# The last row's last local feed-forward and the return of the local stream, as pieces of the last layer's attention part

## The chip, the cores and the metric

The kernel runs on one core of a Trainium2 chip. The metric is the device time of one execution in microseconds (us), of which the median of several runs is taken; lower is better. A traced execution gives the span of the core's instructions and the rows that are quoted here. Engines: PE is TensorE (PEld its weight loads), DVE is VectorE, ACT is ScalarE, POOL is GpSimd, SP is SyncE, which here only issues DMAs.

## The reference

The program is four layers on a residual `x` of shape (4, 512, 128): each adds a cross attention to a context of 77 tokens and then a feed-forward of its own kind. The change touches the feed-forward of layer 2, which is a local transformer of six layers (`DEPTH`), and the cross attention of layer 3 behind it. Cut to what matters:

```python
def attn_layer(x, Wqkv, qs, ksc, Wo): ...      # 16 heads of 64, windows of 32 tokens

def ffn_layer(x, g, bln, W1, b1, W2, b2):
    mu = x.mean(-1, keepdims=True)
    var = ((x - mu) ** 2).mean(-1, keepdims=True)
    xn = (x - mu) / jnp.sqrt(var + 1e-05) * g + bln
    hg = xn @ W1 + b1                           # 128 -> 2 * 341
    a, gate = jnp.split(hg, 2, -1)
    return a * jax.nn.gelu(gate, approximate=False) @ W2 + b2

# _L2_ffn_ref, y = layernorm(x)
for i in range(6):
    y = attn_layer(shift_tokens(y), ...) + y
    y = ffn_layer(shift_tokens(y), ...) + y
x = x + y

# layer 3
x = x + cross_attention(layernorm(x), ctx)      # 16 heads of 8, 77 keys
x = x + routed_experts(layernorm(x))            # 8 experts, the best 2 for each token
```

`shift_tokens` moves the upper 64 features of every token by one token.

## The kernel before, in words

**Data.** A *row* is one of the 4 batch entries `b`. `x[b]` holds a row token-major: 128 partitions of tokens, `NT` = 4 tiles, 128 features. The local transformer keeps its own stream `Y[b]` feature-major, 128 features by 513 columns; its upper 64 features stand one column to the right, so that a slice from column 0 is the shifted stream and a slice from column 1 the unshifted upper half. `middle_part` fills `Y` from the normalised `x`. After the local transformer, `x` receives `Y` back, turned.

**Local transformer** (`local_transformer`). Its order is written out by hand, under `manual_schedule`: a pipeline over 96 tiles (layer, row, tile of 128 tokens), in which pass `n` does the projections of tile `n`, the scores of tile `n-1` and the averages of tile `n-2`. The feed-forward of a row (`ff_stage`) is spread over four passes: moments and normalisation (`ff_moments`, `ff_norm`), turning and gates (`ff_turn`, `ff_gate`), the other half (`ff_up`), and the down product with its add into `Y` (`ff_down`, `add_y` L1717). The row of number `m` has passes `n = 4m + 6` to `4m + 9`. The loop runs 10 passes beyond the 96 tiles. The last two tiles are finished in passes 96 and 97; row 3 of layer 5 (the last) has its feed-forward in passes 98 to 101, when no tile is left. Then a loop over the four rows turns `Y[b]` back with PE in two halves (L2108, 64 features each, since they differ by a column) and DVE adds each half to `x[b]` (L2111).

**Last part** (`last_part`). It is planned: `plan.add` records pieces with what they depend on, the buffers and PSUM banks that they take and use, and a cost for each engine that may do them. `Plan.run` then lists them, always the piece that can start first, the longest path first among equals, and picks the engine where there is a choice. The result is one fixed order per engine; an engine runs its instructions in this order and waits where one isn't ready. `context` forms the keys and values of layer 3 (L636, L649, L640, L657), `cross_attention` goes over the four rows: normalisation (`norm` L535 to L551, transposes L569), queries L684, scores L699 and L704 and their maxima L712, transposes of the maxima L729 and `shift` L738, logits L756 and L758, exponentials L764, the sums `total` L774, the weighted values L783, the projection and the residual L838. `Routing.row` places the tokens with the experts and sends them by indirect DMAs that POOL issues (L1018). In the same plan SP loads the expert weights (L1646 to L1648), and DVE splits `b2` into three bf16 terms (L322 to L329).

Each phase opens its own PSUM pool (`banks`), whose eight banks come free when the phase before has done with them. SBUF pools close with their phase: a later tile may lie where an earlier one was, and then waits for its last user. Before, `Y`'s pool closes with the local transformer, and the tiles of `open_cross` lie over it.

Of the kernel before, what the change touches and what calls it, by code (L numbers as in the profile page):

```python
# [29 lines left out]
NT = S // 128  # L30
# [209 lines left out]
def tile_kernel(ctx: ExitStack, tc: tile.TileContext, A: dict, out: bass.AP):  # L240
# [45 lines left out]
    def p_tr(*shape):  # L286
        return psum(shape, "tr", 2)
# [14 lines left out]
    def copy(e, dst, src):  # L302
        (e.copy if e is SC else e.tensor_copy)(dst, src)
# [223 lines left out]
    def norm(plan, b, after, dst, name, twice=False):  # L527
# [5 lines left out]
        def find(e):  # L533
            for t in range(NT):
                e.bn_stats(st.t[:, t], x[b][:, t])  # L535
            for t in range(NT):
                e.bn_aggr(mv.t[:, t], st.t[:, t])
# [10 lines left out]
        def apply(e):  # L548
            d = dst.t if isinstance(dst, Slot) else dst
            for t in range(NT):  # L550
                e.tensor_scalar(  # L551
                    d[:, t], x[b][:, t], mv.t[:, t, 0:1], rs.t[:, t : t + 1],
                    ALU.subtract, ALU.mult,
                )

        p = plan.add(find, after, takes=[st, mv], V=124)
        p = plan.add(inverse, [p], takes=[rs], uses=[mv], G=135)
        takes = [dst] if isinstance(dst, Slot) else []
        return plan.add(apply, [p], takes=takes, uses=[mv, rs], V=112, G=175)
# [1068 lines left out]
    def last_part():  # L1628

        with ExitStack() as es:  # L1630
# [6 lines left out]
            with tc.tile_pool(name="xw3", bufs=2) as wp, planned() as plan:  # L1637
                keys = context(plan, wp, 2)
                done = cross_attention(plan, wp, 2, keys, [[]] * B)
# [56 lines left out]
    def local_transformer(Y):  # L1696
        with ExitStack() as es:
# [28 lines left out]
            def load(i):  # L1726
# [16 lines left out]
                w1 = wp.tile([128, 2 * DI], F32, name="lw1")  # L1743
                DMA.dma_start(w1, A["L2_ffn_W1"][i])
                w2 = wp.tile([128, 3, D], F32, name="lw2")
# [217 lines left out]
            def ff_turn(F):  # L1963
# [7 lines left out]
                F.h = tp.tile([128, 3, S], F32, name="fh", bufs=1)  # L1971
# [62 lines left out]
            for n in range(len(tiles) + 10):  # L2034
# [66 lines left out]
                if F:  # L2101
                    ff_stage(F, phase, True)

            for b in range(B):
                for r, o in ((slice(0, 64), 0), (slice(64, 128), 1)):
                    t = p_tr(128, NT, 64)
                    for tt in range(NT):
                        PE.transpose(  # L2108
                            t[:, tt], Y[b][r, 128 * tt + o : 128 * tt + o + 128], ident[r, r]
                        )  # L2110
                    V.tensor_tensor(x[b][:, :, r], x[b][:, :, r], t, ALU.add)  # L2111

    with tc.tile_pool(name="y", bufs=1) as yp:
# [9 lines left out]
        local_transformer(Y)  # L2123
    with ExitStack() as es:
        open_cross(es)
        last_part()
# [19 lines left out]
```

## Time and profile before

| | us |
|---|---|
| median of 3 runs | 2501.84 |
| lowest and highest | 2493.18, 2504.8 |
| profiled execution, whole | 2497.58 |
| its span | 2495.8 |
| local transformer, first to last projection (L1780) | 533.7 to 2150.7 |
| row 3's feed-forward of layer 5, from its first transposes | 2188.47 to 2211.86 |
| `Y` turned back, up to the first product of `context` | 2211.87 to 2216.27 |
| attention part of layer 3, to the last row's residual | 2216.27 to 2352.95 |
| mean granted clock of PE over the span | 0.951 |

Times of rows are microseconds from the start of the span. A row of a stage has the stretch, its length, the busy time of PE, PEld, DVE, ACT and POOL with instruction counts, the granted PE clock as a share of full speed, the busy share of the DMA engines, and GB/s. A row of the chain of waits has start, length and what the chain went through. One of the timeline has start, length, engine, line, operation, output and inputs, and in brackets the idle time before it with what ended it. An fp32 matmul counts as two instructions on PE.

### The profile page before, as it was taken

The numbers are of one execution on the slowest core, as the hardware profiler recorded it, in microseconds if no ns is written. First come the engines' busy times: TensorE is split into PE (matmuls) and PEld (weight loads), VectorE is DVE, ScalarE is ACT, GpSimd is POOL, SyncE is SP. The second block draws the span as 40 slices with busy tenths as digits, with TensorE's granted clock in tenths as the row PEclk, the third lists the DMA queues.
The fourth block names the chain that finished last, engine by engine and source line by source line (L and its number), as shares of the span: only waits on it lengthen the run. The fifth ranks groups of instructions, "written<-read, shape, count | busy, mean of one in ns | idle before, by whom it ended". The sixth has DMA issues, their size and how long they took to land.

```text
span 2495.8 us, 86737 instructions
## 1 busy us (share of the span) xinstructions
PE 2257.5 (90%) x37341; PEld 1487.1 (60%) x37341; DVE 1746.9 (70%) x3818; ACT 1292.4 (52%) x2379; POOL 1383.5 (55%) x1948
## 2 busy tenths in 40 slices
PE   7959879968999999999999999999999999978676
PEld 3537644536666666666666666666666666634365
DVE  5526355757788787778888888788788888655522
ACT  3513225545666556666666666556556666524232
POOL 2241232347667666676667766766667666432433
PEclk9959889989999999999999999999999999979788
DMA  6210110014411121111211121111211111111022
GB/s 162 84 39 23 37 42 2 1 49 95 120 34 35 30 57 50 27 35 35 69 35 35 30 76 35 30 31 39 65 35 35 33 29 35 29 39 47 21 74 83
DMA packets 134297, 116.14 MB, mean 47 GB/s; under 512 B 29505, under 2 KB 102700, under 8 KB 133916
## 3 DMA queue, kind: packets, MB, share of 16 engines
q1 hardware_dynamic: 128373, 102.81, 15.8%
q0 software_dynamic: 4608, 7.35, 0.9%
q8 instruction: 296, 4.85, 0.8%
q14 instruction: 85, 0.70, 0.1%
q10 hardware_dynamic: 935, 0.43, 0.1%
HBM read 42.84 MB, written 21.52 MB: 26 GB/s over the span
## 4 chain that ended last, share of the span: by engine, by line
PE 72%; DVE 15%; issue 4%; ACT 3%; DMA 2%; POOL 2%; another core or an unknown queue 2%; SPq 1%; POOLq 0%; ACTq 0%; DVEq 0%
PE ps_tr L583 12%; PE ps_mm L1780 10%; PE ps_av L1942 6%; PE ps_av L1918 5%; PE ps_tr L1857 5%; PE ps_sc L1887 4%; DVE xn L523 3%; PE ps_sc L1977 3%; PE ps_sc L1988 3%; PE ps_sc L2000 2%; PE ps L774 2%; PE ps L1313 2%; PE ps L783 2%; PE ps L1682 2%
## 5 line engine op out<-in xcount | busy, mean ns | idle before, releaser
L1803 POOL TENSOR_TENSOR rc<-rc,rs 128x512 f32<-128x512 f32 x384 | 489.5, 1276 | 385.4 <-DVE rs L1793 329.5
L1780 PE MATMUL ps_mm<-wqk,y 128*128 128x512 f32 x768 | 396.9, 599 | 10.5 <-DVE rs L1793 7.3
L1822 POOL TENSOR_TENSOR rc<-rc,rn_y 128x512 f32<-128x512 f32 x384 | 388.7, 1044 | 7.5
L1790 DVE TENSOR_TENSOR rc<-ps_mm,tabs 128x512 f32<-128x512 f32 x384 | 262.5, 684 | 137.8 <-ACT sq L1782 123.4
L1782 ACT ACTIVATE sq<-ps_mm 128x512 f32<-128x512 f32 x384 | 231.4, 603 | 166.9 <-PE ps_mm L1780 119.3
L1793 DVE TENSOR_TENSOR rs<-ps_mm,tabs 128x512 f32<-128x512 f32 x384 | 261.5, 681 | 1.6 <-POOL rc L1803 1.4
L1802 DVE TENSOR_REDUCE ss<-sq 128x8 f32<-128x512 f32 x384 | 259.5, 676 | 0.0
L583 PE MATMUL ps_tr<-cst,rc 128*128 128x128 f32 x1536 | 210.7, 280 | 6.8 <-issue 4.1
L1918 PEld LDWEIGHTS ps_av<-v,PT 64*32 64x32 f32 x12288 | 138.1, 105 | 124.5 <-PE ps_tr L583 55.8
L1942 PE MATMUL ps_av<-aT,wo 128*128 128x128 f32 x1536 | 199.6, 283 | 3.4 <-issue 3.2
L1942 PEld LDWEIGHTS ps_av<-aT,wo 128*128 128x128 f32 x1536 | 181.0, 193 | 12.7 <-issue 4.0
L583 PEld LDWEIGHTS ps_tr<-cst,rc 128*128 128x128 f32 x1536 | 164.6, 141 | 26.7 <-issue 4.7
L1918 PE MATMUL ps_av<-v,PT 64*32 64x65 f32 x12288 | 169.9, 225 | 4.6 <-DVE attn L1928 2.1
L1887 PE MATMUL ps_sc<-kT,qT 64*32 64x64 f32 x12288 | 146.8, 224 | 28.9 <-issue 26.8
L1018 POOL DMA_INDIRECT back<-ye,to x80 | 78.0, 975 | 162.0 <-DVE ye L1132 120.4
L1887 PEld LDWEIGHTS ps_sc<-kT,qT 64*32 64x32 f32 x12288 | 140.1, 105 | 39.1 <-issue 31.4
L1780 PEld LDWEIGHTS ps_mm<-wqk,y 128*128 128x128 f32 x768 | 124.6, 192 | 60.7 <-issue 48.8
L764 ACT ACTIVATE P<-ps,deltaT 77x512 f32<-77x512 f32 x192 | 115.4, 682 | 77.5 <-PE ps L758 69.9
L1903 ACT ACTIVATE P<-P 128x1024 f32<-128x1024 f32 x96 | 101.5, 1057 | 92.1 <-DVE P L1898 92.1
L1814 ACT ACTIVATE rn_y<-ss 128x32 f32<-128x32 f32 x96 | 22.0, 229 | 238.4 <-POOL ss L1813 238.4
L1834 ACT COPY qT<-ps_tr 128x512 f32<-128x512 f32 x192 | 103.3, 589 | 74.6 <-PE ps_tr L583 74.3
L1834 ACT COPY kT<-ps_tr 128x512 f32<-128x512 f32 x192 | 103.3, 589 | 66.2 <-PE ps_tr L583 65.9
(394 smaller groups left out, 4439.6 us busy)
## 6 DMA issues: line engine op xcount, KB each, us to landing
v<-v SPq DMA_DIRECT2D x432, 65.0 KB
v<-v SPq DMA_DIRECT2D x96, 195.0 KB
wqk<-in_L_ffn_Wqkv_dram SPq DMA_DIRECT2D x24, 256.0 KB
sent<-xn SPq DMA_DIRECT2D x2, 2210.0 KB
xe<-sent SPq DMA_DIRECT2D x16, 260.0 KB
back<-xn SPq DMA_DIRECT2D x2, 2048.0 KB
raw<-in_L_ffn_W_dram SPq DMA_DIRECT2D x8, 512.0 KB
yb<-back SPq DMA_DIRECT2D x16, 256.0 KB
```

Source lines behind the costliest of these rows:

```text
L583: PE.transpose(t[:, i], src[:, i], ident)
L1780: PE.matmul(t, lhs, T.w[2 * kind + c], start=True, stop=True)
L1782: SC.activation(sq, t, AF.Square)
L1790: V.tensor_tensor(a, t, bc(T.tabs[:, 2 * kind, tt], [128, 8, LD], 1), ALU.mult)
L1793: V.tensor_tensor(r.rearrange("p h (x d) -> p h x d", x=2), t.rearrange("p h (x d) -> p h x d", x=2)[:, :, ::-1], bc(T.tabs[:, 2 * kind + ...
L1802: V.tensor_reduce(T.ss[:, kind, 8 * c : 8 * c + 8], sq, AX.X, ALU.add)
L1803: G.tensor_tensor(a, a, r, ALU.add)
L1822: G.tensor_tensor(a, a, bc(y[:, o : o + 8], [128, 8, LD], 2), ALU.mult)
L1834: SC.copy(t[:, 4 * c : 4 * c + 4, lead:], to_features(T.rot[kind, c].rearrange("p (k x) d -> p k (x d)", x=2)),)
L1887: PE.matmul(T.banks[32 * w : 32 * w + 32, z, k], T.qT[r, k, 32 * w : 32 * w + 32], T.kT[r, k, 32 * w : 32 * w + 64], start=False, stop=Tru ...
L1918: PE.matmul(T.means[32 * w : 32 * w + 32, x0, k], T.PT[r, 4 * g + k, 32 * w : 32 * w + 32], (T.v1 if w % 2 else T.v2)[r, x0, 4 * g + k], s ...
L1942: PE.matmul(t, T.wo[:, c], T.aT[:, c], start=(c == 0), stop=(c == 7))
```

## The change

Three things, all at the seam between the local transformer and the last part.

- The loop of the local transformer runs 2 passes beyond the tiles in place of 10. The feed-forward of the last row in the last layer is no longer in it; `last_feed_forward` records it as pieces of the last part's plan: transposes, copy, `norm` (which can now take a source other than `x[b]`), transposes and scaling, gates, Gelu, ups, product, down product, and add into `Y`.
- The loop that turned `Y` back is gone. `add_local` records for each row a piece for PE (both halves, in two banks) and one for DVE (both adds). They are the `start` of the rows in `cross_attention`; row 3's stands behind the feed-forward.
- `lw1`, `lw2` and `fh` come from a pool `lf` that outlives the local transformer, as does the pool of `Y`, so the last part's tiles no longer lie over `Y`.

The diff, cut to its core:

```diff
@@ -524,15 +524,16 @@
                 dst[:, t], src[:, t], mv[:, t, 0:1], rs[:, t : t + 1], ALU.subtract, ALU.mult
             )
 
-    def norm(plan, b, after, dst, name, twice=False):
+    def norm(plan, b, after, dst, name, twice=False, src=None):
 
         st = plan.buf(small, [128, NT, 6], F32, f"{name}_st")
         mv = plan.buf(small, [128, NT, 2], F32, f"{name}_mv")
         rs = plan.buf(small, [128, NT], F32, f"{name}_rs")
 
         def find(e):
+            v = src.t if src else x[b]
             for t in range(NT):
-                e.bn_stats(st.t[:, t], x[b][:, t])
+                e.bn_stats(st.t[:, t], v[:, t])
             for t in range(NT):
                 e.bn_aggr(mv.t[:, t], st.t[:, t])
 
@@ -546,17 +547,18 @@
             e.tensor_tensor(rs.t, rs.t, mhalf[:, :NT], ALU.pow)
 
         def apply(e):
-            d = dst.t if isinstance(dst, Slot) else dst
+            d, v = dst.t if isinstance(dst, Slot) else dst, src.t if src else x[b]
             for t in range(NT):
                 e.tensor_scalar(
-                    d[:, t], x[b][:, t], mv.t[:, t, 0:1], rs.t[:, t : t + 1],
+                    d[:, t], v[:, t], mv.t[:, t, 0:1], rs.t[:, t : t + 1],
                     ALU.subtract, ALU.mult,
                 )
 
-        p = plan.add(find, after, takes=[st, mv], V=124)
+        seen = [src] if src else []
+        p = plan.add(find, after, takes=[st, mv], uses=seen, V=124)
         p = plan.add(inverse, [p], takes=[rs], uses=[mv], G=135)
         takes = [dst] if isinstance(dst, Slot) else []
-        return plan.add(apply, [p], takes=takes, uses=[mv, rs], V=112, G=175)
+        return plan.add(apply, [p], takes=takes, uses=[mv, rs] + seen, V=112, G=175)
 
     def features(plan, src, after, dst, cost=54, idt=None, dtype=None, rows=128, evacuate=None, width=128):
 
@@ -1625,7 +1627,7 @@
                     plan.add(low, [p], uses=[bank], S=59, V=69)
                     plan.add(high, [p], uses=[bank], S=59, V=69)
 
-    def last_part():
+    def last_part(lf, Y, weights):
 
         with ExitStack() as es:
             pool = lambda name, bufs=2: es.enter_context(tc.tile_pool(name=name, bufs=bufs))
@@ -1636,7 +1638,10 @@
             R = Routing(mp, wr[:, 1], CAP3, True)
             with tc.tile_pool(name="xw3", bufs=2) as wp, planned() as plan:
                 keys = context(plan, wp, 2)
-                done = cross_attention(plan, wp, 2, keys, [[]] * B)
+                start = [[add_local(plan, Y, b, [])] for b in range(B - 1)]
+                p = last_feed_forward(plan, lf, Y, weights)
+                start.append([add_local(plan, Y, B - 1, [p])])
+                done = cross_attention(plan, wp, 2, keys, start)
                 for b in range(B):
                     R.row(plan, b, [done[b]])
                 for e0 in range(E):
@@ -1693,7 +1698,8 @@
                     plan.add(store, last[b], Q=40)
 
 
-    def local_transformer(Y):
+    def local_transformer(Y, lf):
+
         with ExitStack() as es:
             es.enter_context(banks())
             es.enter_context(tc.manual_schedule())
@@ -1740,9 +1746,9 @@
                     )
                 wo = wp.tile([128, 8, D], F32, name="wo")
                 DMA.dma_start(wo, A["L2_ffn_Wo"][i].rearrange("(c p) d -> p c d", p=128))
-                w1 = wp.tile([128, 2 * DI], F32, name="lw1")
+                w1 = lf.tile([128, 2 * DI], F32, name="lw1")
                 DMA.dma_start(w1, A["L2_ffn_W1"][i])
-                w2 = wp.tile([128, 3, D], F32, name="lw2")
+                w2 = lf.tile([128, 3, D], F32, name="lw2")
                 DMA.dma_start(
                     w2[:, 0:2], A["L2_ffn_W2"][i][0:256].rearrange("(c p) d -> p c d", p=128)
                 )
@@ -1968,7 +1974,7 @@
                 SC.activation(
                     F.xnT, t, AF.Identity, scale=col(R_LG + F.i), bias=col(R_LB + F.i)
                 )
-                F.h = tp.tile([128, 3, S], F32, name="fh", bufs=1)
+                F.h = lf.tile([128, 3, S], F32, name="fh", bufs=1)
 
             def ff_gate(F, *chunks):
                 t = pair("sc")
@@ -2031,7 +2037,7 @@
             tabs = {0: tables(loaded[0][5])}
             swap(0)
             SC.preload_act_table_set(EXP_LN)
-            for n in range(len(tiles) + 10):
+            for n in range(len(tiles) + 2):
                 T = tiles[n] if n < len(tiles) else None
                 T1 = tiles[n - 1] if 0 <= n - 1 < len(tiles) else None
                 T2 = tiles[n - 2] if 0 <= n - 2 < len(tiles) else None
@@ -2100,17 +2106,103 @@
                     values(T, 1)
                 if F:
                     ff_stage(F, phase, True)
-
-            for b in range(B):
-                for r, o in ((slice(0, 64), 0), (slice(64, 128), 1)):
-                    t = p_tr(128, NT, 64)
-                    for tt in range(NT):
-                        PE.transpose(
-                            t[:, tt], Y[b][r, 128 * tt + o : 128 * tt + o + 128], ident[r, r]
-                        )
-                    V.tensor_tensor(x[b][:, :, r], x[b][:, :, r], t, ALU.add)
-
-    with tc.tile_pool(name="y", bufs=1) as yp:
+            return loaded[DEPTH - 1][3:5]
+
+    def last_feed_forward(plan, lf, Y, weights):
+
+        w1, w2 = weights
+        i, b, chunks = DEPTH - 1, B - 1, range(3)
+        bank, raw = plan.bank(), plan.buf(lnp, [128, NT, D], F32, "xn")
+
+        def flip(e):
+            for t in range(NT):
+                e.transpose(bank.view(128, NT, 128)[:, t], Y[b][:, 128 * t : 128 * t + 128], ident)
+
+        def out(e):
+            copy(e, raw.t, bank.view(128, NT, 128))
+
+        p = plan.add(flip, takes=[bank], PE=54)
+        p = plan.add(out, [p], takes=[raw], uses=[bank], S=59, V=69)
+        xn = plan.buf(lnp, [128, NT, D], F32, "xn")
+        p = norm(plan, b, [p], xn, "yn", src=raw)
+        xnT = plan.buf(lnp, [128, NT, 128], F32, "xnT")
+
+        def scaled(e, dst, src):
+            e.activation(dst, src, AF.Identity, scale=col(R_LG + i), bias=col(R_LB + i))
+
+        p, q = features(plan, lambda: xn.t, [p], xnT, evacuate=scaled)
+        xn.users.append(q)
+        h = plan.buf(lf, [128, 3, S], F32, "fh", 1)
+        gates, ups, sum_ = ([plan.bank() for _ in c] for c in (chunks, chunks, [0]))
+
+        def product(o, banks_):
+            def run(e):
+                for c in chunks:
+                    n, a = CH_W[c], o + 128 * c
+                    e.matmul(
+                        banks_[c].view(n, S), w1[:, a : a + n], xnT.t.rearrange("p a b -> p (a b)"),
+                        start=True, stop=True,
+                    )
+
+            return run
+
+        def gelu(e):
+            for c in chunks:
+                n = CH_W[c]
+                e.activation(
+                    h.t[:n, c], gates[c].view(n, S), AF.Gelu,
+                    bias=col(R_B1 + (3 + c) * DEPTH + i)[:n],
+                )
+
+        def times(e):
+            for c in chunks:
+                n = CH_W[c]
+                e.scalar_tensor_tensor(
+                    h.t[:n, c], ups[c].view(n, S), col(R_B1 + c * DEPTH + i)[:n], h.t[:n, c],
+                    ALU.add, ALU.mult,
+                )
+
+        def down(e):
+            for c in chunks:
+                n = CH_W[c]
+                e.matmul(
+                    sum_[0].view(128, S), w2[:n, c], h.t[:n, c], start=(c == 0), stop=(c == 2)
+                )
+
+        def add(e):
+            for r, o in ((slice(0, 64), 0), (slice(64, 128), 1)):
+                dst = Y[b][r, o : o + S]
+                e.scalar_tensor_tensor(
+                    dst, sum_[0].view(128, S)[r], col(R_B2 + i)[r], dst, ALU.add, ALU.add
+                )
+
+        g = plan.add(product(DI, gates), [p], takes=gates, uses=[xnT], PE=284)
+        u = plan.add(product(0, ups), [p], takes=ups, uses=[xnT], PE=284)
+        p = plan.add(gelu, [g], takes=[h], uses=gates, S=330)
+        p = plan.add(times, [p, u], uses=ups + [h], V=215)
+        p = plan.add(down, [p], takes=sum_, uses=[h], PE=284)
+        return plan.add(add, [p], uses=sum_, V=152)
+
+    def add_local(plan, Y, b, after):
+
+        halves = [plan.bank(), plan.bank()]
+
+        def flip(e):
+            for r, o in ((slice(0, 64), 0), (slice(64, 128), 1)):
+                for tt in range(NT):
+                    a = 128 * tt + o
+                    e.transpose(halves[o].view(128, NT, 64)[:, tt], Y[b][r, a : a + 128], ident[r, r])
+
+        def add(e):
+            for o in range(2):
+                v = x[b][:, :, 64 * o : 64 * o + 64]
+                e.tensor_tensor(v, v, halves[o].view(128, NT, 64), ALU.add)
+
+        p = plan.add(flip, after, takes=halves, PE=60)
+        return plan.add(add, [p], uses=halves, V=84)
+
+    with ExitStack() as stay:
+        yp = stay.enter_context(tc.tile_pool(name="y", bufs=1))
         Y = []
         for b in range(B):
             y = yp.tile([128, S + 1], F32, name=f"y{b}", tag=f"y{b}")
@@ -2120,10 +2212,11 @@
             open_cross(es)
             kept = lambda: es.enter_context(tc.tile_pool(name="b1", bufs=1, side="right"))
             middle_part(*first_part(kept), Y)
-        local_transformer(Y)
-    with ExitStack() as es:
-        open_cross(es)
-        last_part()
+        lf = stay.enter_context(tc.tile_pool(name="lf", bufs=2, side="right"))
+        weights = local_transformer(Y, lf)
+        with ExitStack() as es:
+            open_cross(es)
+            last_part(lf, Y, weights)
 
 
 # ---- launch: one core; inputs and outputs as the reference has them ----
```

## The prediction

> **What bounds the kernel now.** I read the page first, then the chain of waits between 2180 and 2390 us (where the diff acts), then the busy time by stage, then the order of each engine's instructions around the seam between the local transformer and the last part.
>
> The page says that TensorE (PE) is the busiest engine and heads the chain that ended last, so time is bought only where PE waits.
>
> ```profile
> PE 2257.5 (90%) x37341; PEld 1487.1 (60%) x37341; DVE 1746.9 (70%) x3818; ACT 1292.4 (52%) x2379; POOL 1383.5 (55%) x1948
> PE 72%; DVE 15%; issue 4%; ACT 3%; DMA 2%; POOL 2%; another core or an unknown queue 2%; SPq 1%; POOLq 0%; ACTq 0%; DVEq 0%
> ```
>
> The chain of waits (start, length, what) shows the feed-forward of row 3 in layer 5 as a single file. Every step of it is followed by a wait for the next engine, from its first transposes (L1955) to the second half of its add (L1717). Then come the transposes back (L2108), then the values of `context` (L649).
>
> ```profile
> 2184.18 2.59 PE ps_sc L2000 x6
> 2187.56 0.77 DVE y L1717
> 2188.47 0.66 PE ps_sc L1955 x4
> ...
> 2194.90 3.80 PE ps_sc L1977 x4
> ...
> 2207.46 2.86 PE ps_sc L2000 x6
> ...
> 2211.10 0.76 DVE y L1717
> 2211.89 0.43 DVE x L2111
> ...
> 2216.27 0.71 PE ps L649 x2
> ```
>
> The busy times by stage (PE, PEld, DVE, ACT, POOL, granted clock) show what that costs. In the 23.6 us of the single file PE works 12.99 and no other engine over 6.03. In the attention stages that follow PE works 20.6 of 23.5 and 24.4 of 29.5 us, so there is little room left, but some.
>
> ```profile
> 2188.40:2212.00 23.60, 12.99 (x34) 4.86 (x34) 6.03 (x18) 5.88 (x7) 2.60 (x9) 0.78 0.03 7
> 2216.00:2237.00 21.00, 19.59 (x106) 9.94 (x106) 15.53 (x78) 3.89 (x9) 14.04 (x18) 0.59 0.09 29
> 2237.00:2260.50 23.50, 20.55 (x303) 10.73 (x299) 17.52 (x52) 11.40 (x19) 4.18 (x5) 1.00 0.32 92
> 2260.50:2290.00 29.50, 24.41 (x325) 12.56 (x324) 23.83 (x89) 12.21 (x21) 4.31 (x12) 0.94 0.13 32
> 2318.50:2352.50 34.00, 28.17 (x281) 14.57 (x281) 12.46 (x60) 11.62 (x20) 14.07 (x22) 0.75 0.06 18
> ```
>
> Landmarks from the timeline: values of `context` start at 2216.27, the first `maxes` of row 0 (L712) at 2228.59, and the residuals of rows 0 to 3 (L838) at 2260.56, 2289.88, 2318.58 and 2352.27.
>
> **The change, part by part.** The order of the instructions in the two built programs is the same on every engine up to the down product of row 2 (L2000 at 2184), also for the loads of `lw1` and `lw2` from their new pool. So the edit to the pools, and the eight passes of the loop that are gone, cost nothing before that point.
>
> 1. *The single file goes.* From 2188.47 to 2211.86: -23.4 us.
>
> 2. *Turning back.* It took 2211.87 to 2216.27, 4.4 us, for four rows. Now only row 0's eight transposes (0.5 us, as at 2210.24) stand before `context`: -3.9 us. The first of them waits until DVE has read the old PSUM banks (L1717, 2188.3), as L1955 does now, so that wait is no new cost. The transposes of rows 1 and 2, and the four of row 3's feed-forward, stand between the keys and row 0's normalised transposes, where PE waits for DVE anyway (0.14 us each, 24 in 3.39 us with waits: about 3 us). The cover is the 8 us of DVE and POOL work in step 3; without it 3 us more.
>
> 3. *Row 0 starts less well.* DVE now has the biased keys `kT` (L640) ahead of row 0's statistics, and POOL has two of the `km` products ahead of row 0's inverse root. Before, row 0's normalisation was done beside the values. From the start of the values: values and keys 6.5 (2216.27 to 2222.76), `kT` 1.2, two `km` on POOL 2.2, inverse root 1.4, apply and transposes 1.3, copy 0.6, queries 2.1, `qT` 0.7, scores 1.4, with 0.05 to 0.1 for each hand-over: 17.7 us to the first `maxes`, against 12.3 now: +5.4 us. These are durations at half clock. The row for 2216 to 2237 has a granted clock of 0.59 (0.50 up to 2232) with PE busy 19.59 of 21.00. The Trainium skill ("TensorE: Matmul & The Clock Gate", Part 1) would have full clock after about 3.4 us of sustained work. By that rule values, keys, transposes and queries take half as long (estimate: 12.5 us instead of 17.7, so +0.2). I take the row: it is the same work, after the same kind of gap (2186.8 to 2188.5), and it stayed at half for 20 us.
>
> 4. *The feed-forward's work now lies in the attention stages.* PE: three gates 2.85, three ups 2.85 (L1988, 1.95 and 1.09 with gaps out), down 2.6, eight transposes 1.3: 9.6 us. The gates stand in PE's queue ahead of row 0's `maxes` transposes (L729), which every later step of row 0 waits for: 2.85. Ups and down stand ahead of row 0's projection and row 1's logits: 5.45. Row 3's normalisation is applied on POOL, not on DVE (four times 0.79 us by L551, against 1.11 in all), ahead of row 1's and row 2's. PE, in order, waits for row 2's transposes before row 1's scores and the gates: I take 1 us, between 0 and the 3.2 that POOL is held. Sum +9.3. ACT's part (copy, `xnT`, three Gelus, two table loads of 1.28) is 5.9 us and DVE's (statistics, three products, two adds) 4.9 us. The table loads, gone from the single file, come back here, the second ahead of row 0's first exponential. I take both at nothing, since ACT works 11.4 of 23.5 us and waits for PE. Uncovered they would cost up to 10.8.
>
> 5. *DVE's splitting of `b2`* (L322 to L329, seven instructions, about 1.95 us a time). Weights are loaded once PE's L1942 is done (2184) instead of L2000 (2210; SP waited 44.8 us for it), into a DMA system that is at 0.00 to 0.03 busy there, so two of the eight go ahead of row 0's `shift` and all eight ahead of row 0's residual. Before, four lay between 2261 and 2274, one directly ahead of row 1's `shift`, for which PE then waits 2.43 us. I take -3 for rows 1 to 3 (between 0 and -7.8, four of them). Their delay of row 0 is taken as beside the gates and row 1's scores.
>
> 6. *POOL's and DVE's blanking.* `vpad` (1.80 us, at 2215.82 only after L2108 had read Y) gets other memory and goes to 2186, beside L2000, off row 0's inverse root: in step 3 already.
>
> Row 3's stream is ready after step 4, some 30 us before its scores: no cost. The stages after 2352 have the same work and move as a whole.
>
> Sum: -23.4 - 3.9 + 5.4 + 9.3 - 3 = -15.6, about **-16 us**. The profiled execution took 2497.58 us (span 2495.8), so 2481.6 for such an execution. It lies 4.3 below the median of the runs, 2501.84, so about 2486 for a median. Half a percent (12.5 us) is about what a measurement of this kernel can tell from no change.
>
> **The rivals.**
>
> *All of it is hidden (-21 to -27).* PE is idle 3 to 6 us in each attention stage, and clock and splitting may fall well: step 3 at +0.2 gives -21, step 4 at 4 instead of 9.3 a further 5. For: the idle time is there. Against: gates, ups and down stand in queue ahead of exactly the steps that a row waits for.
>
> *It comes back inside the attention part (-9 to 0).* ACT's and DVE's shares in step 4 turn out on the path too (10.8 us): -5. For: row 0's `shift` now stands behind two splittings and four `maxes` of row 1 on DVE. Against: in the same stretch PE has work of row 1.
>
> *Slower, by PE starved under the sends.* While POOL issues the indirect sends (L1018, eight of 1.27 us), groups of `total` (L774, normally 1.08 us) came in pieces. Row 2's second took 2296.71 to 2301.9 and one of row 3's 2329.81 to about 2337, some 4 and 6 us too long, with "issue" ahead of each piece.
>
> ```profile
> 2329.81 0.82 PE L774 MATMUL ps<-P,onep 77*32 77x128 f32 x9
> 2331.07 0.44 PE L774 MATMUL ps<-P,onep 77*32 77x128 f32 x5 [0.44 <-issue]
> 2332.54 1.12 PE L774 MATMUL ps<-P,onep 77*32 77x128 f32 x5 [1.03 <-issue]
> ```
>
> Two groups suffer now. Eight stand in rows 2 and 3. At 5 us each, three more give the 16 us back, and six more make it 14 us slower. For: in the new order row 0's sends come while row 2's groups run. Against: one run of eight sends is over in 10.2 us and at 2326.22 a group under them took 1.08. That the change doesn't do what it says is excluded: the built order has the pieces where step 4 puts them.
>
> **How the numbers follow.** -16 us (from -10 to -21): 0.62. All hidden: 0.12. Given back inside: 0.19. Slower: 0.07. Of the likeliest case about 0.09 falls short of 12.5 us. So faster by over 0.5%: 0.53 + 0.12 = 0.65; within: 0.09 + 0.19 = 0.28; slower: 0.07. Range: from all hidden (2501.84 - 27 = 2475) to nearly all given back (-2, 2500).
>
> **What would show it.** Right: after row 2's L1717 PE goes on with row 0's transposes within 0.3 us; first `maxes` of row 0 near 2207 (2202 with the clock up); residual of row 0 near 2247, the last near 2337; the whole tail moved by one amount; clock 0.5 from 2189 to about 2209. Wrong: row 0's residual later than 2255 (step 4 too small), or `total` of rows 2 and 3 in pieces more than twice (the third rival), or the tail from 2382 on longer than 113.8 us.

## The result, and the profile after

The changed kernel takes 2478.22 us (median of 6 runs, 2475.2 to 2479.44), the kernel before 2499.51 beside it (6 runs, 2493.18 to 2504.8). The ratio is 0.9908, 95% interval 0.989 to 0.9926: faster by 0.7 to 1.1%. Timed a second time it took 2491.81 against 2512.38, a ratio of 0.9928 (0.9904 to 0.9952). So the medians moved by 20.6 to 21.3 us; the prediction had said 16 less.

The page of the changed kernel: PE still leads, and its share of the chain is 71 instead of 72%.

```profile
PE 2242.8 (91%) x37341; PEld 1478.8 (60%) x37341; DVE 1745.4 (71%) x3818; ACT 1291.9 (52%) x2379; POOL 1383.7 (56%) x1948
PE 71%; DVE 15%; issue 4%; DMA 3%; POOL 3%; ACT 2%; another core or an unknown queue 1%; SPq 1%; POOLq 0%; DVEq 0%; ACTq 0%
```

The chain of waits around the seam (start, length, what). Line numbers are those of the changed kernel: two more than before in the attention part, six more in the local transformer; L2194 and L2199 are the flip and the add of `add_local`, L2142 the gates and ups, L2168 the down product.

```profile
2172.71 2.59 PE ps_sc L2006 x6
2175.31 0.03 issue
2175.33 0.74 DVE y L1723
2176.07 0.01 issue
2176.09 0.77 DVE y L1723
2176.86 0.14 issue
2176.99 0.47 PE ps L2194 x8
2177.47 0.37 PE ps L651 x2
...
2181.63 1.34 PE ps L638 x2
...
2183.06 1.17 DVE kT L642 x4
2184.22 0.09 issue
2184.31 2.15 POOL km L659 x2
2186.47 0.08 issue
2186.55 0.24 POOL xa_rs L546
...
2189.39 3.46 POOL xn L552 x4
...
2194.28 3.14 POOL xa_n L552 x4
...
2198.85 3.15 POOL xa_n L552 x4
2202.00 0.04 issue
2202.05 0.33 PE ps L571
...
2209.14 1.85 PE ps L686 x2
```

Three things are to be seen. Behind row 2's add (L1723) PE goes straight on with row 0's flip and the values of `context`: the single file is gone. Then `kT` and two `km` stand ahead of row 0's inverse root (`xa_rs`), as step 3 said. And then POOL, applying three normalisations one after the other (9.75 us), is the chain until 2202. PE works beside most of that: it waits for POOL's tiles 1.70 us in all, two times for row 1's and two times for row 2's. Row 2's 0.90 us are what step 4 had taken at 1. In the timeline of PE:

```profile
2196.70 0.33 PE L571 MATMUL ps<-cst,xa_n 128*128 128x128 f32 x1 [0.35 <-POOL xa_n L552]
2197.48 0.33 PE L571 MATMUL ps<-cst,xa_n 128*128 128x128 f32 x1 [0.45 <-POOL xa_n L552]
...
2201.27 0.33 PE L571 MATMUL ps<-cst,xa_n 128*128 128x128 f32 x1 [0.45 <-POOL xa_n L552]
2202.05 0.33 PE L571 MATMUL ps<-cst,xa_n 128*128 128x128 f32 x1 [0.45 <-POOL xa_n L552]
```

The 6.8 us left out between the last two lines of the chain are scores, maxima and two of DVE's splittings of `b2`.

By stage (the stretch, its length, busy PE, PEld, DVE, ACT, POOL, granted clock, DMA share, GB/s), from the values to the first `maxes`, from there to row 0's residual, and the two stretches up to the residuals of rows 2 and 3:

```profile
2177.40:2194.80 17.40, 13.55 (x67) 7.44 (x68) 11.15 (x55) 3.39 (x8) 9.92 (x13) 0.54 0.27 80
2194.80:2236.00 41.20, 37.05 (x383) 17.28 (x383) 31.79 (x93) 18.23 (x28) 7.00 (x10) 0.95 0.24 65
...
2262.00:2299.70 37.70, 32.17 (x335) 17.36 (x334) 18.49 (x71) 11.65 (x20) 15.26 (x25) 0.80 0.05 15
2299.70:2328.00 28.30, 22.90 (x267) 12.33 (x266) 9.84 (x42) 11.34 (x20) 9.28 (x10) 0.79 0.06 20
```

In row 0 PE now works 37.05 of 41.20 us and DVE 31.79. The two profiles' spans differ by 22.4 us, but **the local transformer's last projection already starts 11.5 us earlier** in the profile after, in code whose order is the same. So the first question is which part of the gain belongs to the change.

### The profile page after: what moved, and what is told of

It reads as the page before. It is cut to its first block, busy times and chain, and to the rows that moved or that the text cites. A ratio compares the mean times of both kernels' runs of the same rounds, so it can differ in the third digit from the quotient of the medians.

```text
span 2473.4 us, 86733 instructions
## 1 busy us (share of the span) xinstructions
PE 2242.8 (91%) x37341; PEld 1478.8 (60%) x37341; DVE 1745.4 (71%) x3818; ACT 1291.9 (52%) x2379; POOL 1383.7 (56%) x1948
## 4 chain that ended last, share of the span: by engine, by line
PE 71%; DVE 15%; issue 4%; DMA 3%; POOL 3%; ACT 2%; another core or an unknown queue 1%; SPq 1%; POOLq 0%; DVEq 0%; ACTq 0%
PE ps_tr L585 12%; PE ps_mm L1786 11%; PE ps_av L1948 6%; PE ps_av L1924 5%; PE ps_tr L1863 5%; PE ps_sc L1893 4%; DVE xn L523 3%; PE ps_sc L1994 2%; PE ps_sc L2006 2%; PE ps_sc L1983 2%; PE ps L776 2%; PE ps L1315 2%; PE ps L1687 2%; PE ps L785 2%; PE ps L1571 1%
## 5 line engine op out<-in xcount | busy, mean ns | idle before, releaser
L1020 POOL DMA_INDIRECT back<-ye,to x80 | 78.0, 975 | 160.3 <-DVE ye L1134 117.7
L766 ACT ACTIVATE P<-ps,deltaT 77x512 f32<-77x512 f32 x192 | 115.0, 684 | 69.2 <-PE ps L760 61.8
L1909 ACT ACTIVATE P<-P 128x1024 f32<-128x1024 f32 x96 | 101.5, 1057 | 90.9 <-DVE P L1904 90.9
```

## The experiments

All landmarks, in us, from the timelines. "Last projection" is its start (L1780 in before), "to context" runs from there to the first product of the values, "to maxima" from there to row 0's first `maxes`, "row 0" from there to its residual, "rows" from the residual of row 0 to that of row 3, "tail" from there to the end, and "behind" is the sum of the five. (The expectations quoted below count from the squaring of the last projection on ACT, 0.7 us later. In them e1_pools is the kernel with the pools alone, e7_b2 the one with `b2` later, e8_fill the one with PE filled.) Every kernel but before and after has one profile.

| kernel | last projection | to context | to maxima | row 0 | rows | tail | behind | ratio to before (95%) |
|---|---|---|---|---|---|---|---|---|
| before | 2150.7 | 65.6 | 12.3 | 32.0 | 91.7 | 143.5 | 345.1 | |
| before, again | 2138.5 | 70.8 | 12.3 | 31.5 | 92.6 | 143.5 | 350.7 | |
| after | 2139.2 | 38.2 | 17.4 | 41.2 | 91.9 | 145.6 | 334.2 | 0.9908 (0.989 to 0.9926) |
| after, second profile | 2150.8 | 38.4 | 17.6 | 39.7 | 92.6 | 144.5 | 332.9 | |
| after, third profile | 2142.9 | 39.0 | 16.4 | 40.1 | 91.5 | 145.1 | 332.1 | 0.9928 (0.9904 to 0.9952) |
| pools alone | 2148.0 | 69.2 | 12.3 | 31.7 | 98.3 | 144.3 | 355.8 | 0.9989 (0.9974 to 1.0004) |
| turning in pieces alone | 2154.5 | 67.0 | 18.0 | 31.5 | 101.7 | 144.3 | 362.5 | 1.0018 (1.0005 to 1.003) |
| feed-forward alone | 2154.4 | 41.5 | 13.1 | 46.8 | 89.4 | 146.3 | 337.1 | 0.9929 (0.9903 to 0.9956) |
| no feed-forward | 2153.8 | 38.5 | 17.6 | 31.5 | 95.3 | 145.2 | 328.1 | 0.9885 (0.9864 to 0.9906) |
| feed-forward later | 2158.8 | 40.3 | 16.9 | 36.1 | 101.5 | 146.5 | 341.3 | 0.9946 (0.9926 to 0.9967) |
| keys later | 2152.5 | 38.4 | 17.7 | 40.6 | 92.1 | 142.8 | 331.7 | 0.9919 (0.9891 to 0.9947) |
| `b2` later | 2148.3 | 38.4 | 17.4 | 35.4 | 99.4 | 144.5 | 335.1 | 0.9921 (0.9896 to 0.9946) |
| PE filled | 2145.3 | 38.2 | 14.8 | 40.9 | 91.8 | 144.9 | 330.6 | 0.9906 (0.9881 to 0.993) |
| PE filled, `b2` out | 2159.1 | 38.7 | 15.7 | 37.4 | 90.8 | 149.2 | 331.7 | 0.9931 (0.9904 to 0.9958) |

**Is the time ahead of the seam the change's?** Both kernels were profiled again without an edit, the changed one also timed again.

> The kernel before once more, for its profile alone. In the profiles of before and after the local transformer, whose instructions and order are the same in both, begins (first projection) at 533.7 and at 524.5 us, and its last projection at 2150.7 and 2139.2: 11.5 us of the 22.4 between the two spans lie ahead of the changed part. Theory 'chance' (the granted clock falls differently from execution to execution): this profile may begin it anywhere between about 522 and 536, and one of the two new profiles moves by more than 4 us. Theory 'placement' (the new pools move addresses, and the program then always takes another course): 533 to 535 again, last projection 2149 to 2152.

> The changed kernel once more, for its profile alone. 'Chance': first projection of the local transformer anywhere between 522 and 536. 'Placement': 523.5 to 525.5, last projection 2138 to 2141. Behind the last projection both theories expect what the first profile had: 334 us from the last projection to the end, against 345 in before.

> The changed kernel once more, timed as often as the others. From the last projection of the local transformer to the end it took 333.5 and 332.2 us in two profiles, before 344.4 and 350.0: 14.5 less on the mean. Theory 'chance': the time ahead of the last projection scatters by some 12 us in both kernels alike, so the median settles 13 to 17 below before's, near 2486. Rival: the first comparison, 21 us, was no accident, and it stays near 2478.

The rows of the projection (duration min, median and max, first and last start) in the second profile of before, then the first and the second of after:

```profile
L1780 PE MATMUL ps_mm<-wqk,y x768: 590/592/1222, 524.1 to 2138.5; 128*128 128x512 f32 x192
```

```profile
L1786 PE MATMUL ps_mm<-wqk,y x768: 590/592/1220, 524.5 to 2139.2; 128*128 128x512 f32 x192
```

```profile
L1786 PE MATMUL ps_mm<-wqk,y x768: 590/592/1222, 529.1 to 2150.8; 128*128 128x512 f32 x192
```

Before now reaches its last projection at 2138.5, as the first profile of after did, and after at 2150.8, as before did. Over all 14 profiles of the table, which share the code up to there, the last projection starts between 2138.5 and 2159.1, in both kinds of kernel: chance, some 20 us wide. It is seen in the clock: from 20 to 420 us the granted clock of PE is 0.87 in the two profiles that come late (before and the second of after) and 0.90 in the two that come early; behind 420 it is 0.99 in all four. By estimate the 0.03 of 400 us are 12 us. At the first projection, though, the late ones are behind by only 9.6 and 4.6 us, so this isn't all of it. The two first profiles' 22.4 us are therefore 11.5 of chance and 10.9 behind it. With the other profiles the way behind the last projection is 347.9 on the mean before (two) and 333.1 after (three): -14.8, and the nearest two profiles of the two kernels are 10.9 apart. The third expectation named 13 to 17 for the medians; 20.6 was measured, with an interval of about 12 to 24 us, so it is neither confirmed nor excluded.

**Do the pools alone do anything?**

```diff
-    def local_transformer(Y):
+    def local_transformer(Y, lf):
-                w1 = wp.tile([128, 2 * DI], F32, name="lw1")
+                w1 = lf.tile([128, 2 * DI], F32, name="lw1")
...
+    with ExitStack() as stay:
+        yp = stay.enter_context(tc.tile_pool(name="y", bufs=1))
```

> Before, with the pools alone of the change: lw1, lw2 and fh in a pool that stays open, and the pool of Y open to the end. Loop and turning back as before. 'Placement': first projection near 524.5, last near 2139, and a time of about 2488 (11 us less than before). 'Chance': no time from it ahead of the changed part on average, so 2496 to 2500: at most 3 us of gain, from the blanking of vpad and from the splitting of b2, which move. In both the way from the last projection to the end should be 342 to 346 us, since the feed-forward of row 3 is still a single file.

Ratio 0.9989, and 1 is in the interval: no gain that can be measured. "Placement" is out. The profiled execution was long behind the last projection (355.8), against the expectation: its rows took 98.3, with a granted clock of 0.5 from 2301.8 to 2322.3, where before has it from 2301.6 to 2305.0. So a single profile's rows can be 6 us off by the clock alone, in an order that no edit changed.

**Turning in pieces alone, and the feed-forward alone.** The first leaves row 3's feed-forward in the loop and plans the turning of all four rows; the second plans the feed-forward and turns rows 0 to 2 by hand as before.

```diff
# turning alone, against after
-            for n in range(len(tiles) + 2):
+            for n in range(len(tiles) + 10):
-                start = [[add_local(plan, Y, b, [])] for b in range(B - 1)]
-                p = last_feed_forward(plan, lf, Y, weights)
-                start.append([add_local(plan, Y, B - 1, [p])])
+                start = [[add_local(plan, Y, b, [])] for b in range(B)]
# feed-forward alone, against after
+            for b in range(B - 1):
+                for r, o in ((slice(0, 64), 0), (slice(64, 128), 1)):
...
-                start = [[add_local(plan, Y, b, [])] for b in range(B - 1)]
+                start = [[] for b in range(B - 1)]
```

> The change without its largest part: the feed-forward of row 3 stays in the loop as a single file, and all four rows are turned back by planned pieces (new pools as in the change). By the prediction's steps 2 and 3, -3.9 for the turning and +5.4 for the worse start of row 0: +1.5 behind the last projection, so 345 to 348 us from it to the end, and the time of e1_pools plus 1 or 2. Rival: turning back in pieces is a gain by itself, 340 to 342 us from the last projection to the end.

> The feed-forward of row 3 planned as in the change, but rows 0 to 2 turned back by hand ahead of the plan, as before (row 3 in pieces). Theory A (turning in pieces costs more at the start of row 0 than it brings): 3.3 us of turning come back, 5.4 at the start of row 0 and some at the later rows go, so 2 to 6 us faster than the changed kernel; values of context to first maxima 12 to 13 us, against 17.5. Theory B (the start is late because of the feed-forward's pieces, not of the turning): maxima still at 16 to 18, and 3 us slower than the changed kernel.

Turning in pieces alone is slower than before (1.0018, interval above 1), and by 8 us slower than the pools alone (medians 2506.65 and 2498.48), where 1 or 2 were expected. Context starts 2.2 us sooner than with the pools alone, and the stage up to the first maxima takes 5.7 us longer, near the -3.9 and +5.4 of steps 2 and 3. The rest of the 8 is open: the 3.4 us more in the rows are no measure of it, since the half clock falls differently in the two profiles (row 3 at 0.59 here, at 0.80 there). So the whole gain is the feed-forward's. Yet the feed-forward alone is no better than the full change (0.9929 against 0.9928): the first maxima are as early as theory A said (13.1), but row 0 takes 46.8 instead of 40.3. Both theories missed: the 4 us won at the start were handed back within the same row. Two things lie in it, and no run takes them apart. On DVE a splitting of `b2` stands ahead of row 0's `shift` (PE waits 1.72 us for it) and two more ahead of its residual. And the granted clock of row 0 is 0.88 instead of 0.95 to 1.00: the half clock runs from 2195.9 to 2216.4, and as the start is shorter, 7.4 us of it fall into row 0.

**The price of the feed-forward's pieces.**

```diff
-                p = last_feed_forward(plan, lf, Y, weights)
-                start.append([add_local(plan, Y, B - 1, [p])])
+                start.append([add_local(plan, Y, B - 1, [])])
```

> The changed kernel with the feed-forward of row 3 in layer 5 left out altogether (its stream is turned back without it): the price of its pieces in the attention part. By step 4 of the prediction 9.3 us less than the changed kernel, nearly all of it between the first maxima and the residual of row 1: 32 instead of 40 to 41 us from first maxima to the residual of row 0, or the same sum spread over rows 0 and 1. Rival (all hidden): 0 to 3 us less. Rival (dearer than PE's part, ACT's 5.9 and DVE's 4.9 uncovered too): 12 to 20 less.

Row 0 falls from 40.3 (mean of three) to 31.5: 8.8 us, of the 9.3 predicted, and all of it in row 0. By the medians, timed side by side, it is 8.6 (2491.81 and 2483.18). Behind the last projection this one profile has 5.0, since its rows take 95.3 instead of 92.0. Without the feed-forward three of the eight splittings of `b2` fall into row 1, with it none.

**The feed-forward later.** Cut to its core:

```diff
-        p = plan.add(flip, takes=[bank], PE=54)
+        p = plan.add(flip, after, takes=[bank], PE=54)      # after row 0's L731
```

> The changed kernel with the feed-forward of row 3 held until the maxima of row 0 are transposed; nothing else. Theory A (step 4: the gates' 2.85 us and PE's wait for POOL's normalisation lie on row 0's path, and POOL's 3.5 us ahead of the normalisation of rows 1 and 2): first maxima to the residual of row 0 falls from 40 to 41 us to 34 to 37, 3 to 5 us faster in all. Theory B (PE is full anyway, the work only moves to where it delays rows 1 or 2 by as much): row 0 earlier, the residual of row 3 not; within 2 us of the changed kernel.

Row 0 gained 4.2, and the rows lost 9.5 (row 1 alone 31.9 instead of 25.9 to 26.7): a ratio of 0.9946, the highest of those that plan the feed-forward, but its interval overlaps with that of after. Theory B, and by this profile worse than it said. Why row 1 pays more than row 0 gains was not tried; its granted clock is 0.89, against 0.94 to 1.00 in after.

**The keys later.** `kT` waits for row 0's normalised tiles, whose normalisation is recorded first; gates and ups are tied to their places, and the copies into `vpad` stay on ACT. Cut to its core:

```diff
-        k = plan.add(biased, [p], takes=[kT], uses=[kb], V=100)
+        k = plan.add(biased, [p, *behind], takes=[kT], uses=[kb], V=100)   # behind: row 0's apply
-        g = plan.add(product(DI, gates), [p], takes=gates, uses=[xnT], PE=284)
+        g = plan.add(product(DI, gates), [p, scored], takes=gates, uses=[xnT], PE=284)
```

> The changed kernel with the biased keys kT (and so the km products) held until row 0's normalised tiles are written; the gates are held until row 0's last scores and the ups until its last averages, so that PE's order stays nearly that of the changed kernel. Theory of step 3 (kT on DVE ahead of row 0's statistics and two km on POOL ahead of its inverse root cost the 5 us): values of context to first maxima falls from 16.4 to 17.6 to 12.5 to 14.5, the whole by 3 to 4 us. Rival (the keys are needed just as soon, and end last instead of the queries): 16 to 17.5 again, no gain.

No gain: 17.7, as the rival said. The timeline of PE shows row 0's tiles turned early, and then the scores waiting for the one `km` that is left on POOL, which stands behind row 3's normalisation (chain: `xn`, 3.35 us):

```profile
2200.66 1.15 PE L571 MATMUL ps<-cst,xa_n 128*128 128x128 f32 x4 [1.83 <-DVE xa_n L552]
2202.49 2.07 PE L690 MATMUL ps<-xa_t,wT 128*128 128x512 f32 x2 [0.67 <-ACT xa_t L303]
...
2207.49 0.80 PE L710 MATMUL ps<-km,qT 32*128 32x308 f32 x8 [1.67 <-POOL km L659]
```

So the order on DVE was not the whole cause: with it eased, the queue of POOL took over.

**DVE's splitting of `b2`.**

```diff
-                    plan.add(terms, [p], uses=[row], V=120)
+                    plan.add(terms, [p, done[0]], uses=[row], V=120)
```

> The changed kernel with DVE's splitting of b2 held until the residual of row 0, where four of the eight were before the change. Step 5 of the prediction (early splitting buys rows 1 to 3 3 us): the residuals of rows 0 and 3 lie 95 us apart instead of 91.5 to 92.6, 3 us slower. Rival (DVE had the time, early splitting brings nothing): 92 us apart again, and row 0 up to 2 us earlier, since one group stands ahead of its first maxima and three ahead of its shift.

Both are partly right. Row 0 falls by 4.9 to 35.4, more than the rival's 2, and the rows grow by 7.4 to 99.4, more than step 5's 3. Together it costs 2.5 by the profiles; the ratio (0.9921) can't tell that. The row of PE (row 2's queries) that waits for row 1's maxima behind two splittings, in the third profile of after and here:

```profile
2213.04 1.12 PE L686 MATMUL ps<-xa_t,wT 128*128 128x512 f32 x2 [2.03 <-DVE maxes L714]
```

```profile
2214.83 1.12 PE L686 MATMUL ps<-xa_t,wT 128*128 128x512 f32 x2 [0.56 <-DVE maxes L714]
```

That is 1.5 of the 4.9 us. Another part is not the splitting's own: the plan picks the engine, and with the splitting held it gives row 1's normalisation to DVE instead of POOL (1.12 us instead of 3.14). PE's five waits of 0.45 us for POOL's tiles, which the third profile of after has in row 0, are gone. In the timeline of DVE here:

```profile
2203.08 1.12 DVE L552 TENSOR_SCALAR xa_n<-x,xa_mv,xa_rs 128x128 f32<-128x128 f32 x4 [1.96 <-POOL xa_rs L547]
```

And of the 7.4 us in the rows 3.8 lie in row 2, whose granted clock is 0.66 here and 0.80 in after. Whether the edit did that is not shown, as the pools alone, in the order of before, have 35.6 us at 0.71 for this row, where before has 28.7 at 0.94. Row 2 here, then with the pools alone:

```profile
2266.37:2307.80 41.43, 36.44 (x325) 18.74 (x325) 22.84 (x84) 12.13 (x21) 16.87 (x20) 0.66 0.15 44
```

```profile
2290.35:2325.99 35.64, 30.00 (x297) 15.07 (x296) 13.46 (x49) 10.73 (x19) 8.86 (x11) 0.71 0.05 16
```

Rows 1 and 3 account for the other 3.5, about the 3 of step 5.

**The half clock at the seam.**

```diff
+            t = p_tr(128, NT, 128)                       # behind the loop
+            for k in range(12):
+                PE.transpose(t[:, k % NT], ident, ident)
...
+                def fill(e):                             # in the plan, read by nothing
+                    for k in range(20):
+                        e.transpose(spare.view(128, NT, 128)[:, k % NT], ident, ident)
```

> The changed kernel with work added on PE that nothing reads: 12 transposes behind the last down product of the loop, and 20 behind the planned transposes ahead of row 0's normalised tiles, both where PE waited (1.70 and 3.17 us). Theory A (the granted clock halves at the seam because PE is idle there, half of one 3.4 us slice and 86% of another): no or one slice of half clock at the seam instead of four or five, and values of context to first maxima 12.5 to 14 us instead of 16.4 to 17.6, as by the skill's rule in step 3; 3 to 5 us faster. Theory B (the half clock comes for another reason than those waits): four or five half slices all the same, and up to 2 us slower by the added work.

The two waits of PE in the first profile of after:

```profile
2176.99 0.47 PE L2194 MATMUL ps<-cst,y 64*128 64x64 f32 x8 [1.70 <-DVE y L1723]
...
2188.43 1.15 PE L571 MATMUL ps<-cst,xa_n 128*128 128x128 f32 x4 [3.17 <-DVE xa_n L552]
```

With PE filled 0.39 and 1.75 us of them are left. The stage from the values on, in the second profile of after and with PE filled (here the stretch ends 2.7 us behind the first maxima):

```profile
2190.00:2207.30 17.30, 13.47 (x65) 7.50 (x68) 10.93 (x56) 3.39 (x8) 10.36 (x14) 0.51 0.28 81
```

```profile
2184.40:2201.00 16.60, 11.95 (x90) 7.13 (x90) 13.05 (x60) 3.39 (x8) 11.80 (x16) 1.00 0.27 83
```

The granted clock is 1.00 instead of 0.51 over the stage, and one slice of 3.4 us at half is left (2202.4 to 2205.8) where the three profiles of after have 17.1, 17.0 and 13.6 us. Theory A, with less gain than it named: first maxima at 14.8 instead of 17.1 (mean), since what DVE, POOL and ACT do there hardly gets shorter (11.16, 9.25 and 3.36 us up to the first maxima, against 11.16, 9.94 and 3.39 in after), and the added transposes take room. The ratio, 0.9906, can't be told from the changed kernel's own.

**Both together.** Two of the splittings of `b2` stand behind row 3 and six behind the routing's totals, on top of the filled PE. Cut to its core:

```diff
-                    row = plan.buf(wp, [128, D], F32, "b2f")
+                    row = plan.buf(wp, [128, D], F32, "b2f", E)
-                    plan.add(terms, [p], uses=[row], V=120)
+                    plan.add(terms, [p, done[B - 1] if e0 < 2 else counted], uses=[row], V=120)
```

> The changed kernel with the added transposes of e8_fill, and with all of DVE's splitting of b2 taken out of the attention part: two of the eight groups behind the residual of row 3 and six behind the routing's totals, where DVE waited 12.29 us for the sent rows (b2's raw terms get a buffer for each expert, so that the loading of the weights doesn't wait for them). PE's order stays that of e8_fill. Theory (two groups ahead of row 1's maxima hold PE in row 0, as e7_b2's 5 us showed, and the later ones hold the shift of rows 1 to 3, as its rows showed): first maxima to the residual of row 0 falls to 35 to 36.5 us, the residuals of rows 0 and 3 lie at most 92 us apart, and the way behind the last projection is 322 to 326 us instead of 329.9: a ratio of about 0.988. Rival (the splitting was beside other work there, and e7_b2's row 0 gained for another reason): 329 to 331 us again.

Row 0 fell by 3.5 against PE filled and the rows by 1.0, about as the theory said (37.4, 90.8), and the tail gave 4.3 back: 331.7, the rival's number without the rival's reason. DVE was idle there, but not free of waiters. The timeline of DVE, then that of POOL:

```profile
2350.29 0.35 DVE L329 SCALAR_TENSOR_TENSOR b<-tt_low,cst,tt_acc 128x128 bf16<-128x128 f32 x1
2350.56 0.18 DVE L916 TENSOR_REDUCE pm<-ps 128x4 f32<-128x32 f32 x1
...
2375.65 1.40 DVE L1083 SCALAR_TENSOR_TENSOR xe<-xe,free,xe 128x130 f32<-128x130 f32 x5 [3.78 <-DMA xe<-sent]
```

```profile
2354.35 0.97 POOL L1020 DMA_INDIRECT sent<-rows,place  x1 [0.30 <-issue]
2358.10 0.97 POOL L1020 DMA_INDIRECT sent<-rows,place  x1 [2.78 <-DVE pl L981]
```

Row 3's routing (L916) now stands directly behind the second splitting, and POOL waits 2.78 us for its places; in after it waits 1.84. The last splitting ends at 2370.7, and only then does SP issue the loads of `xe` (chain: L1051 at 2370.88). From the last send's end to the first `xe` it takes 7.5 us, in after 4.5. Row 0's granted clock is 0.92 besides, with half from 2209.5 to 2219.7, so the filling did not keep the clock up in this profile as it did alone. No complete version in the table is shown to beat the changed kernel.

## Why the prediction was right, point by point

The forecast (-16, faster by more than 0.5% at 0.65) holds: -14.8 behind the last projection by five profiles, -20.6 and -21.3 by the medians. The 6 us between the two measures stay open. Two profiles of before are few for a way that took 345.1 in one and 350.7 in the other. That the sum is so near is luck in part: against the steps the misses are -2.4, -0.6, -0.8, +2.9 and +1.6, and they cancel.

1. *The single file goes* and 2. *turning back*: predicted -27.3, measured -27.4 between the first two profiles (65.6 to 38.2). On the mean of all it is -29.7. The term was sized on a fast execution: in the other one the half clock of the single file lasted 20.5 us (2178.5 to 2202.4, with a break) instead of 10.3 (2188.9 to 2199.2), and the way to context took 70.8. As announced, PE goes on 0.14 us behind row 2's add.
3. *Row 0's start*: predicted 17.7, measured 17.4, 17.6 and 16.4 (+4.8 on the mean, for +5.4). Taking the row and not the rule was right here: the Trainium skill ("TensorE: Matmul & The Clock Gate", Part 1) has full clock after about 3.4 us of sustained work, and here the half began at 2178.7 and lasted 17.1 us, although PE worked without a wait from 2176.99 to 2185.26; in the other two profiles it lasted 17.0 and 13.6. The mechanism was only half right. With `kT` held back the start stayed at 17.7, since POOL's queue then held the keys.
4. *The feed-forward's work*: predicted +9.3, measured +8.5 in row 0 (31.8 to 40.3 on the mean), and 8.8 without the pieces. Size and place are right, the make-up isn't. Row 0 takes 31.5 with four of the splittings and without the feed-forward, 35.4 the other way round, and 40.3 with the feed-forward and seven splittings. So the feed-forward without the splitting is only 3.9 above the 31.5, and the other 4.9 come with the splitting and with the normalisation that the plan then leaves on POOL. (A kernel with neither was not run.) PE's wait for row 2's tiles was sized rightly, 0.90 for 1; its waits for row 1's, 0.80, were not counted. That the 9.3 nearly came out is luck in part: 4.9 of it go with the splitting, which step 5 put at nothing.
5. *`b2`*: predicted -3 for the rows and nothing for row 0. **This is the step that failed.** The delay of row 0, put at nothing, is 4.9 us with what the plan moves along with it (`b2` later). The prediction took it as covered by the gates and row 1's scores. These do run beside it, but in the first profile of after they are through at 2207.1, and then PE's queue has row 2's queries, which wait 2.02 us for row 1's maxima, and these stand behind two splittings. The cover ended before the delay did. For the rows, 92.0 instead of 92.2 us is nothing, yet row 1 did fall by 3.1 (26.2 from 29.3), where the wait of 2.43 us for its `shift` is gone, as the step said. Row 2 grew by 8.9 (37.6 from 28.7) and row 3 fell by 5.9 (28.3 from 34.2). Together these two take 3.0 more, with the granted clock of row 2 at 0.80 instead of 0.94; no run tells why.
6. *The tail*: predicted 0, measured +1.6 on the mean. From the first `xe` to the end the first profile has 115.7 us, 1.9 beyond the 113.8 that were named as a sign of error. What lengthens it wasn't tried.

The rivals: "all hidden" is excluded by the 8.8 us of the feed-forward. "Given back inside" is true in part, 14.9 us of the 29.7 come back (4.8 at the start, 8.5 in row 0, 1.6 in the tail), and its cause, DVE ahead of row 0's `shift` and maxima, was seen at work. "PE starved under the sends" did not grow in number: again two groups came in pieces, one of row 2 and one of row 3. The first of them, in the timeline of PE:

```profile
2274.25 0.63 PE L776 MATMUL ps<-P,onep 77*32 77x128 f32 x13
2275.89 0.43 PE L776 MATMUL ps<-P,onep 77*32 77x128 f32 x5 [1.01 <-issue]
2277.35 0.42 PE L776 MATMUL ps<-P,onep 77*32 77x128 f32 x4 [1.03 <-issue]
```

It lies where row 0's eight sends do (POOL, L1020, 2268.7 to 2278.8), and the half clock of that stage begins in it (2277.7 to 2291.3; in before it lasts 3.4 us behind row 2's group in pieces). So its price may have grown. This was read only; no run took the sends away.

## What to carry to other kernels

Moving a single file into a planned stage pays even when half of what it saves comes back on the path, because the file with the turning took 27.8 us, of which PE worked 16.34 (2188.47 to 2216.27 in before). But ask of each moved piece what stands behind it in the other engines' queues: POOL's normalisations, DVE's splitting and the keys took turns as the last wait, and freeing one (keys later, `b2` out) handed the bound to the next. A plan that picks the engine also moves other pieces when one is held, so look at what moved before a gain is put down to the piece. And take a stage's own time from several profiles, with its granted clock beside it, before a difference is believed: here half of the first difference of spans was chance in code that the change didn't touch.

## What the runs showed of the hardware

The granted clock of PE moves in slices of 3.4 us, and at the seam it fell behind waits of PE, not behind work. In the profile after, the first half slice follows the slice from 2175.3 to 2178.7, of which PE waited 1.70 us; with both waits of the seam shortened (to 0.39 and 1.75 us) by transposes that nothing reads, the stage kept 1.00. How long the half then lasts is not told by the last slice alone: 13.6 to 17.1 us after, 20.5 before (2212.8 to 2233.3), with PE busy most of it. The same four normalising instructions took 3.14 to 3.46 us on POOL and 1.11 on DVE.

The time up to the last projection scatters by 20 us between executions of the same instructions, and the profiles differ in where the half clock falls between 130 and 350 us: in before from 134.1 to 192.1 in one piece, in after with a break from 144.3 to 154.6.
